# Norm roots on GpSimd, one scaling of the adjacency, a bf16 one-hot, and three VectorE steps on ScalarE, in a four-layer graph network

## The chip, the cores and the metric

The kernel runs on one core of one Trainium2 chip. The metric is the device time of one launch in microseconds, the median of three runs. Engines are named as the profile names them: PE (TensorE; PEld its weight loads), DVE (VectorE), ACT (ScalarE), POOL (GpSimd) and SP (SyncE, which issues all DMAs here).

## The reference

64 graphs of 256 nodes with 128 features go through four layers. The adjacency is 0 or 1, symmetric, with ones on its diagonal, and about one entry in eight is set. Each layer's result is added to its input and normalised over the features.

```python
# layer 0: for each node, the maximum over its neighbours
pre = p[:, :, None, :] + q[:, None, :, :] + b      # p = x (W1 - W2), q = x W2
x = ln(x + max(relu(pre) * adj[..., None], axis=2))
# layer 1: three representations (elu), two aggregated over adj, concatenated
x = ln(x + tanh(concat([adj @ in_rep, node_rep, adj.T @ out_rep]) @ W_upd.T + b_upd))
# layer 2: two graph convolutions with a normalised adjacency
A_hat = adj + eye; deg = A_hat.sum(-1); dinv = where(deg > 0, rsqrt(deg), 0)
norm_A = dinv[..., :, None] * A_hat * dinv[..., None, :]
h = elu(elu(x @ W0 + b0))
h = elu(norm_A @ (h @ W1) + b1)
x = ln(x + norm_A @ (h @ W2) + b2)
# layer 3: a message for every pair, summed over neighbours, and an update
msg = gelu(ln(m_j[:, None] + m_i[:, :, None] + b1) * g1 + be1)
agg = einsum('bijo,bij->bio', msg, adj)
x = ln(x + ln(concat([x, agg]) @ W2 + b2) * g2 + be2)
```

The outer norm is `(x - mean) / sqrt(var + 1e-5)`.

## The kernel before

One graph is one tile of work: its 256 nodes are two halves (`H = 2`) of 128 partitions. The kernel has a path for sparse adjacencies (`sparse`), which this input takes, and a general path behind a flag (`general`), which is built but not run here.

The sparse path doesn't go over all pairs. For each half of the neighbours and each node it lists the neighbours by rank in 40 slots; the nodes are sorted by their number of neighbours, so that later slots are narrower (`RECTS`, 4800 columns in all). A one-hot matrix `hot` in fp8 picks the neighbours by a matmul: `q3` times `hot` for layer 0 (L665, with `pick`/`lack` matmuls L681 that push empty places down, and `fold` with a maximum, L492) and `c3` times `hot` for layer 3 (L728). In layer 3 `sums_of` makes up to 1024 columns at a time: evict and add `dT` (L732, DVE), square (L736, ACT), sum over the features by a matmul with ones (L743), `row` (L745, ACT), out to DRAM as a `line`, back as 16 columns (`vr`), root, reciprocal and a product with `fulls` (L768, L769), out again (L771) and back as `rs_s`, spread over the partitions (L828). `last` then multiplies (L839, DVE), takes the Gelu (L841, ACT), and folds with a sum.

Each tile goes through four stages: `first` (the sorting, `perm`, `hot`, layer 0), `second` (layer 1), `third` (layer 2 and the start of layer 3) and `last`. Four tiles are under way at a time, one in each stage. `together` takes steps of the four generators in turn by their weights, and a scheduler then orders the instructions of each engine by its own estimates. So the order on an engine is fixed when the program is built, each engine works through its list in order, and an instruction that waits holds all behind it.

The steps that the change touches:

- `inverse_root` (L72 to L75): Sqrt on ACT and reciprocal on DVE, on the spot. It is called by `layernorm` (L176, on `rs`, 128x2; five norms a tile), by `layer_2` (L272, on `dinv`) and by `sums_of` (L768, on `vr`). ACT keeps one table of functions at a time; where the function's table isn't there the profile shows an ACT_TABLE_LOAD with the line of the instruction that follows it. Copy, Identity, Square, Sign, Abs and Relu have no such loads of their own here.
- `layer_2` (L261): degree to `dinv`, the identity added to `aT` in place (L277), and per step the hidden state `hs` multiplied by `dinv` (L293, DVE), the matmul with `aT` (L296, PE), a copy (L299), a matmul, and `dinv` and the bias on the way out (L308).
- `elu` (L187): Exp on ACT (L194), for the first hidden layer a second one (L198), and two DVE instructions (L200, L201).
- `first`: `nz`, the adjacency in bf16 (L509, DVE, from `an` that a DMA brings, L507); `diff`, for the flag (L511); the number of neighbours `pc` (L534); four Sign activations that count a node's place (L551); `perm`, the one-hot of the permutation (L560, DVE), in fp32 and read in bf16 through every second half-word (`as_bf16`, L561); matmuls with it (L566, L577) and the copy `nzp` (L571); `full`, ones where a slot is filled (L615, DVE). `perm` is read in fp32 by `third` (L810).
- `layer_1`: `nd`, the node representation with its bias (L233, DVE), then its `elu`.

Of the kernel before, what the change touches and what calls it, by code (L numbers as in the profile page):

```python
# [9 lines left out]
F32 = mybir.dt.float32  # L10
BF16 = mybir.dt.bfloat16
AF = mybir.ActivationFunctionType
ALU = mybir.AluOpType
# [6 lines left out]
P = 128  # L20
# [23 lines left out]
def kernel(  # L44
# [9 lines left out]
    nc = tc.nc  # L54
    B, N, D = x.shape
    assert N == 2 * P and D == P
    H = N // P
    Q = P // 4

    consts = ctx.enter_context(tc.tile_pool(name="consts", bufs=1))  # L60
# [7 lines left out]
    nc.vector.memset(eps_t, EPS)  # L68
    minus1 = consts.tile([P, 1], F32, name="minus1")
    nc.vector.memset(minus1, -1.0)  # L70

    def inverse_root(t):  # L72

        nc.scalar.activation(t, t, AF.Sqrt)  # L74
        nc.vector.reciprocal(t, t)  # L75
# [29 lines left out]
    b1_node = column(l1_b_node, "b1_node")  # L105
# [16 lines left out]
    with tc.tile_pool(name="prep", bufs=1) as prep, tc.tile_pool(  # L122
        name="ps_prep", bufs=2, space=bass.MemoryType.PSUM
# [33 lines left out]
    class Shared:  # L157
# [53 lines left out]

        def node_tile(self, name):
            return self.state.tile([P, H, P], F32, name=name)

        def layer_1(self, s, an, aT, x1):

            work, psum, elu = self.work, self.psum, self.elu
# [15 lines left out]
            nc.vector.tensor_scalar(nd, pn[:, :N], b1_node, None, ALU.add)  # L233
# [27 lines left out]
        def layer_2(self, s, aT, deg_of):  # L261
# [3 lines left out]
            deg = work.tile([P, H], F32, name="deg")  # L265
            deg_of(deg)
            nc.vector.tensor_scalar(deg, deg, 1.0, None, ALU.add)
            pos = work.tile([P, H], F32, name="pos")
            nc.vector.tensor_scalar(pos, deg, 0.0, None, ALU.is_gt)
            dinv = work.tile([P, H], F32, name="dinv")  # L270
            nc.vector.tensor_scalar(dinv, deg, 1e-30, None, ALU.max)
            inverse_root(dinv)  # L272
            yield
            nc.vector.tensor_mul(dinv, dinv, pos)
            for h in range(H):
                blk = aT[:, h, h * P:(h + 1) * P]
                nc.vector.tensor_add(blk, blk, ident)  # L277
            yield
# [12 lines left out]
            for step in (1, 2):  # L291
                for h in range(H):
                    nc.vector.tensor_scalar(hs[:, h], hs[:, h], dinv[:, h:h + 1], None, ALU.mult)  # L293
# [60 lines left out]
    def sparse(ctx):  # L354
# [14 lines left out]
        iota_k = cs.tile([P, N], F32, name="iota_k")  # L369
        down = cs.tile([1, N], BF16, name="down")  # L370
# [19 lines left out]
        with tc.tile_pool(name="cs_prep", bufs=1) as pp:  # L390
# [7 lines left out]
            nc.vector.tensor_copy(iota_k, t)  # L398
            t = pp.tile([P, 1], I32, name="part_i")
# [73 lines left out]
        def as_bf16(t):  # L473

            return t.bitcast(BF16).rearrange("... (n two) -> ... n two", two=2)[..., 1]
# [26 lines left out]
        def first(g, s):  # L502
# [6 lines left out]
            nc.vector.tensor_scalar(nz, an, 1.0, None, ALU.is_equal)  # L509
# [33 lines left out]
            dg = state.tile([P, H], F32, name="dg", bufs=3)  # L543
            nc.vector.tensor_reduce(dg, pc, AX.X, ALU.add)
            s["dg"] = dg
# [11 lines left out]
            perm = state.tile([P, H, H, N], F32, name="perm", bufs=3)  # L557
            for h in range(H):
                for hi in range(H):
                    nc.vector.tensor_scalar(perm[:, h, hi], iota_k, pos[:, h, hi:hi + 1], None, ALU.is_equal)  # L560
            perm_b = as_bf16(perm)  # L561
# [53 lines left out]
            nc.vector.tensor_scalar(full, lack, 0.0, None, ALU.is_equal)  # L615
# [102 lines left out]
        def sums_of(s, i):  # L718
# [49 lines left out]
            inverse_root(vr[:rows])  # L768
# [13 lines left out]
        def third(g, s):  # L782

            dg = s["dg"]

            def deg_of(deg):
                nc.vector.tensor_scalar(deg, dg, 1.0 / N, None, ALU.mult)

            yield from sh.layer_2(s, s["aT"], deg_of)
            yield  # L790
            x3, perm = s["x3"], s["perm"]
# [103 lines left out]
    def general(ctx):  # L895
# [82 lines left out]
        def middle(g, s):  # L978
# [10 lines left out]
            def deg_of(deg):  # L989
                nc.vector.tensor_reduce(deg, an, AX.X, ALU.add)  # L990

            yield from sh.layer_1(s, an, aT, s["x1"])
            yield
            yield from sh.layer_2(s, aT, deg_of)
# [148 lines left out]
```

## Time and profile before

| | |
|---|---|
| runs | 5717.65, 5735.95 and 5736.4 us, median 5735.95 |
| the profiled execution | 5731.62 us, its span 5729.7 us |
| mean granted TensorE clock | 0.862 |
| PE / DVE / ACT / POOL busy | 4529.9 / 4834.4 / 4275.2 / 1.9 us |
| ACT_TABLE_LOAD, by the line behind it | L841 535, L74 445, L194 221, L198 32; 1283 ns each |
| L74 on `rs`, `vr`, `dinv` | 320, 320 and 64 activations, 0.20 to 0.22 us |
| DMA | 365.15 MB, mean 64 GB/s |

Busy times are sums over the whole span, in which all 64 tiles stand one behind the other, with four under way at a time. PE's is modelled, since matmuls are pipelined. The windows view gives the busy time of each engine in any stretch with the clock that TensorE was granted in it, the timeline gives the instructions in order, with the time that the engine was idle before them and what ended it.

### The profile page before, as it was taken

The page shows a single profiled execution, that of the slowest core. Times are in us where ns is not written, and L with a number is a line of the kernel's source. Part 1 is how long each engine was busy: PE and PEld are TensorE (multiplying, and loading weights), DVE is VectorE, ACT ScalarE, POOL GpSimd, SP SyncE. Part 2 cuts the span into 40 slices and gives each one's busy share as a digit, 9 for nine tenths or more (in the row PEclk, how much of TensorE's full clock was granted, in tenths as well). Part 3 has the DMA queues.
Part 4 walks back from the last instruction along what each step waited for, and adds up shares of the span by engine and source line. Part 5 has one row for each costly group of instructions (what it writes and reads, how often), then busy time and mean ns, then how long its engine had stood idle before and what let it go on. Part 6 is the DMA issues. An engine that isn't in the chain of part 4 may idle for free.

```text
span 5729.7 us, 83531 instructions
## 1 busy us (share of the span) xinstructions
PE 4529.9 (79%) x27408; PEld 2508.7 (44%) x27408; DVE 4834.4 (84%) x14654; ACT 4275.2 (75%) x6485; POOL 1.9 (0%) x10
## 2 busy tenths in 40 slices
PE   5878878878778778788788788787887887877875
PEld 2444444444444444444444444444444444444443
DVE  6788888888888888888888888888888888888876
ACT  2577777777777777777777777777777777777785
POOL 0000000000000000000000000000000000000000
PEclk8888889889889889888898898898888887888986
DMA  0122222222212221221221222122212212221222
GB/s 22 44 70 63 62 63 72 62 63 66 69 57 70 65 63 63 72 63 62 63 72 62 63 65 70 59 68 65 63 62 72 64 62 63 69 66 60 68 65 74
DMA packets 292813, 365.15 MB, mean 64 GB/s; under 512 B 151952, under 2 KB 210448, under 8 KB 292368
## 3 DMA queue, kind: packets, MB, share of 16 engines
q1 hardware_dynamic: 292368, 359.73, 20.0%
q8 instruction: 217, 3.56, 0.3%
q14 instruction: 228, 1.87, 0.1%
HBM read 345.07 MB, written 14.53 MB: 63 GB/s over the span
## 4 chain that ended last, share of the span: by engine, by line
PE 52%; DVE 29%; ACT 11%; issue 4%; DMA 3%; SPq 0%; DVEq 0%; POOL 0%; ACTq 0%
PE bigp L665 11%; PE bigp L728 8%; DVE pre L839 6%; PE mm L860 5%; DVE lanes L492 4%; PE mm L743 4%; DVE hot L629 4%; DVE pre L732 4%; DVE sums L492 3%; PE bigp L681 3%; DMA rs_s<-scale_line 2%; PE mm L870 2%; PE mm L296 2%; PE mm L699 2%; PE mm L647 2%
## 5 line engine op out<-in xcount | busy, mean ns | idle before, releaser
L665 PE MATMUL bigp<-hot,q 128*128 128x512 fp8e4 (+1 forms) x3840 | 1052.3, 371 | 66.6 <-DVE lanes L492 52.6
L728 PE MATMUL bigp<-hot,c 128*128 128x512 fp8e4 (+1 forms) x3840 | 928.8, 372 | 140.2 <-DVE pre L732 140.2
L732 DVE TENSOR_TENSOR pre<-bigp,dT 128x512 f32<-128x512 f32 (+6 forms) x1664 | 846.3, 530 | 37.8 <-PE bigp L728 33.5
L492 DVE TENSOR_TENSOR lanes<-bigp,lanes 128x512 f32<-128x512 f32 (+6 forms) x1536 | 772.7, 503 | 94.6 <-PE bigp L681 86.9
L839 DVE TENSOR_TENSOR pre<-pre,rs_s 128x1024 f32<-128x1024 f32 (+1 forms) x640 | 732.9, 1150 | 48.6 <-DMA rs_s<-scale_line 48.0
L736 ACT ACTIVATE sq<-pre 128x1024 f32<-128x1024 f32 (+1 forms) x640 | 638.5, 998 | 169.9 <-DVE pre L732 163.9
L841 ACT ACT_TABLE_LOAD x535 | 686.4, 1283 | 9.5
L492 DVE TENSOR_TENSOR sums<-pre,sums 128x1024 f32<-128x1024 f32 (+6 forms) x1024 | 628.8, 614 | 41.2 <-ACT pre L841 40.7
L745 ACT ACTIVATE row<-mm,eps_t 128x256 f32<-128x256 f32 (+1 forms) x640 | 289.6, 453 | 476.9 <-PE mm L743 476.7
L841 ACT ACTIVATE pre<-pre,be,g 128x1024 f32<-128x1024 f32 (+1 forms) x512 | 594.2, 1172 | 57.8 <-DVE pre L839 53.0
L743 PE MATMUL mm<-sq,ones 128*32 128x256 f32 (+1 forms) x5120 | 482.9, 440 | 135.2 <-ACT sq L736 135.2
L74 ACT ACT_TABLE_LOAD x445 | 570.9, 1283 | 7.5
L728 PEld LDWEIGHTS <-c 128*128 128x128 bf16 x3840 | 331.2, 98 | 550.5 <-issue 136.1
L665 PEld LDWEIGHTS <-q 128*128 128x128 bf16 x3840 | 310.8, 97 | 392.6 <-issue 112.0
L296 PE MATMUL mm<-aT,hs 128*128 128x256 f32 x512 | 232.3, 600 | 316.1 <-DVE hs L293 214.8
L629 DVE TENSOR_SCALAR hot<-rank 128x512 fp8e4<-128x512 bf16 (+5 forms) x1536 | 440.5, 348 | 0.0
L681 PEld LDWEIGHTS <-pick 42*128 42x128 bf16 x2944 | 155.8, 95 | 481.5 <-issue 474.2
L296 PEld LDWEIGHTS mm<-aT,hs 128*128 128x128 f32 x512 | 135.6, 293 | 425.8 <-issue 316.1
L860 PE MATMUL mm<-w3u,sums 128*128 128x128 f32 x2048 | 296.7, 289 | 18.4 <-DVE sums L492 16.1
L194 ACT ACT_TABLE_LOAD x221 | 283.5, 1283 | 3.9
L681 PE MATMUL bigp<-lack,pick 42*128 42x36 bf16 (+16 forms) x2944 | 285.7, 187 | 0.0
L860 PEld LDWEIGHTS mm<-w3u,sums 128*128 128x128 f32 x2048 | 254.5, 195 | 37.3 <-issue 17.6
(226 smaller groups left out, 7132.6 us busy)
## 6 DMA issues: line engine op xcount, KB each, us to landing
rs_s<-scale_line SPq DMA_DIRECT2D x512, 512.0 KB
rs_s<-scale_line SPq DMA_DIRECT2D x128, 352.0 KB
an<-in_adj SPq DMA_DIRECT2D x64, 256.0 KB
x<-in_x SPq DMA_DIRECT2D x64, 128.0 KB
line<-row SPq DMA_DIRECT2D x512, 4.0 KB
out<-o SPq DMA_DIRECT2D x64, 128.0 KB
fu<-fulls SPq DMA_DIRECT2D x192, 4.0 KB
vr<-line SPq DMA_DIRECT2D x192, 8.0 KB
```

Source lines behind the costliest of these rows:

```text
L74: nc.scalar.activation(t, t, AF.Sqrt)
L492: nc.vector.tensor_tensor(lanes[:, :k, :w], src[:, i:i + k], lanes[:, :k, :w], op)
L629: nc.vector.tensor_scalar(hot[:, :, at:at + w], rank[:, :, :w], s0 + i + 1.0 - FAR, None, ALU.is_equal, saturate=False)
L665: nc.tensor.matmul(pt[:, :tl], q3[:, i, h], hot[:, h, t0:t0 + tl], start=i == 0, stop=False)
L681: nc.tensor.matmul(o_, l_, r_, start=False, stop=i == len(todo) - 1)
L728: nc.tensor.matmul(pt[:, :bl], c3[:, k, h], hot[:, h, t0 + b:t0 + b + bl], start=k == 0, stop=k == 2)
L732: nc.vector.tensor_add(block(pre[:, b:], n, w, at), block(pt, n, w, at), widen(dT[:, h, :w], n))
L736: nc.scalar.activation(sq[:, :tl], pre[:, :tl], AF.Square)
L743: nc.tensor.matmul(pr[q * Q:(q + 1) * Q, :tl // 4], ones[:, :Q], v4[:, :, q], start=True, stop=True)
L839: nc.vector.tensor_mul(pre[:, :tl], pre[:, :tl], rs[:, :tl])
L841: nc.scalar.activation(msg[:, :tl], pre[:, :tl], AF.Gelu, bias=be3, scale=g3)
L860: nc.tensor.matmul(pt[:, cols], lanes[:, k, cols], w3u[:, 1], start=k == 0, stop=False)
```

## The change

Six edits, and what goes with them:

- `inverse_root` becomes one POOL instruction, the power -0.5 (`mhalf` holds the exponents). `vr` keeps Sqrt and reciprocal, now written out in `sums_of`.
- `dinv` is made by a new `inverse_root_of`, in the sparse path in `first` right after `pc`, and kept for `third` (four buffers); its product with `pos` is on POOL.
- In `layer_2` the rows of `aT` are multiplied by `dinv` once per tile, after the identity is added; the two products of `hs` go.
- `perm` is made in bf16 from a bf16 `iota_b`, without the half-word view; `third` makes an fp32 copy `perm_f` on ACT for its matmul.
- `nz` is a copy on ACT instead of a comparison on DVE.
- `nd` is an Identity activation with bias, and `full` a Relu of 1 - `lack`, both on ACT instead of DVE.

```diff
     def inverse_root(t):
-        nc.scalar.activation(t, t, AF.Sqrt)
-        nc.vector.reciprocal(t, t)
+        nc.gpsimd.tensor_tensor(t, t, mhalf[:t.shape[0], :t.free_size()], ALU.pow)
...
+        def inverse_root_of(self, deg, bufs):
+            nc.vector.tensor_scalar(deg, deg, 1.0, None, ALU.add)
+            pos = self.work.tile([P, H], F32, name="pos")
+            nc.vector.tensor_scalar(pos, deg, 0.0, None, ALU.is_gt)
+            dinv = self.state.tile([P, H], F32, name="dinv", bufs=bufs)
+            nc.vector.tensor_scalar(dinv, deg, 1e-30, None, ALU.max)
+            inverse_root(dinv)
+            nc.gpsimd.tensor_mul(dinv, dinv, pos)
+            return dinv
...
             nd = work.tile([P, N], F32, name="nd")
-            nc.vector.tensor_scalar(nd, pn[:, :N], b1_node, None, ALU.add)
+            nc.scalar.activation(nd, pn[:, :N], AF.Identity, bias=b1_node)
...
             for h in range(H):
                 blk = aT[:, h, h * P:(h + 1) * P]
                 nc.vector.tensor_add(blk, blk, ident)
+            for h in range(H):
+                nc.vector.tensor_scalar(aT[:, h], aT[:, h], dinv[:, h:h + 1], None, ALU.mult)
...
             for step in (1, 2):
-                for h in range(H):
-                    nc.vector.tensor_scalar(hs[:, h], hs[:, h], dinv[:, h:h + 1], None, ALU.mult)
                 pa = psum()
...
-            nc.vector.tensor_scalar(nz, an, 1.0, None, ALU.is_equal)
+            nc.scalar.copy(nz, an)
...
-            dg = state.tile([P, H], F32, name="dg", bufs=3)
+            dg = work.tile([P, H], F32, name="dg")
             nc.vector.tensor_reduce(dg, pc, AX.X, ALU.add)
-            s["dg"] = dg
+            nc.vector.tensor_scalar(dg, dg, 1.0 / N, None, ALU.mult)
+            s["dinv"] = sh.inverse_root_of(dg, 4)
...
-            perm = state.tile([P, H, H, N], F32, name="perm", bufs=3)
+            perm = state.tile([P, H, H, N], BF16, name="perm", bufs=3)
             for h in range(H):
                 for hi in range(H):
-                    nc.vector.tensor_scalar(perm[:, h, hi], iota_k, pos[:, h, hi:hi + 1], None, ALU.is_equal)
-            perm_b = as_bf16(perm)
+                    nc.vector.tensor_scalar(perm[:, h, hi], iota_b, pos[:, h, hi:hi + 1], None, ALU.is_equal)
+            perm_b = perm
...
-            nc.vector.tensor_scalar(full, lack, 0.0, None, ALU.is_equal)
+            nc.scalar.activation(full, lack, AF.Relu, bias=one_t[:ROWS], scale=-1.0)
...
-            inverse_root(vr[:rows])
+            nc.scalar.activation(vr[:rows], vr[:rows], AF.Sqrt)
+            nc.vector.reciprocal(vr[:rows], vr[:rows])
...
-            x3, perm = s["x3"], s["perm"]
+            x3 = s["x3"]
+            perm = work.tile([P, H, H, N], F32, name="perm_f")
+            nc.scalar.copy(perm, s["perm"])
```

The general path gets the same `inverse_root_of`; it isn't run here. The constants `mhalf`, `one_t` and `iota_b` are made once.

More of the change, by code (lines that the diff above doesn't have):

```diff
@@ L68 @@
     nc.vector.memset(eps_t, EPS)
+    one_t = consts.tile([P, 1], F32, name="one_t")
+    nc.vector.memset(one_t, 1.0)
     minus1 = consts.tile([P, 1], F32, name="minus1")
     nc.vector.memset(minus1, -1.0)
+    mhalf = consts.tile([P, 16], F32, name="mhalf")
+    nc.vector.memset(mhalf, -0.5)
     def inverse_root(t):
-        nc.scalar.activation(t, t, AF.Sqrt)
-        nc.vector.reciprocal(t, t)
+        nc.gpsimd.tensor_tensor(t, t, mhalf[:t.shape[0], :t.free_size()], ALU.pow)
     def load(src, shape, name):
@@ L259, in layer_1, with layer_2 @@
             s["x2"] = x2
-        def layer_2(self, s, aT, deg_of):
+        def layer_2(self, s, aT, dinv_of):
             work, psum, elu = self.work, self.psum, self.elu
             x2 = s["x2"]
[L265 to L272, printed above, removed]
+            dinv = dinv_of()
             yield
-            nc.vector.tensor_mul(dinv, dinv, pos)
             for h in range(H):
@@ L369, in sparse @@
         iota_k = cs.tile([P, N], F32, name="iota_k")
+        iota_b = cs.tile([P, N], BF16, name="iota_b")
         down = cs.tile([1, N], BF16, name="down")
@@ L398, in sparse @@
             nc.vector.tensor_copy(iota_k, t)
+            nc.vector.tensor_copy(iota_b, t)
             t = pp.tile([P, 1], I32, name="part_i")
@@ L782, in third @@
         def third(g, s):
[L784 to L789, printed above, removed]
+            yield from sh.layer_2(s, s["aT"], lambda: s["dinv"])
             yield
-            x3, perm = s["x3"], s["perm"]
+            x3 = s["x3"]
+            perm = work.tile([P, H, H, N], F32, name="perm_f")
+            nc.scalar.copy(perm, s["perm"])
             x3T = sh.to_features(x3, "x3T")
@@ L987, in middle, with dinv_of @@
             yield
-            def deg_of(deg):
+            def dinv_of():
+                deg = work.tile([P, H], F32, name="deg")
                 nc.vector.tensor_reduce(deg, an, AX.X, ALU.add)
+                return sh.inverse_root_of(deg, 1)
             yield from sh.layer_1(s, an, aT, s["x1"])
             yield
-            yield from sh.layer_2(s, aT, deg_of)
+            yield from sh.layer_2(s, aT, dinv_of)
             yield
```

## Prediction

> **What bounds the kernel now.** I read the totals first, then the windows over one tile's period, then the order of time inside it. A tile's period is the distance between two `nzp` copies (L571): seven of them start at 2925.4 to 3448.6 us, so 523.2 / 6 = 87.2 us; 64 tiles of that and the fill make the span of 5729.7 us. The totals show no full engine:
>
> ```profile
> PE 4529.9 (79%) x27408; PEld 2508.7 (44%) x27408; DVE 4834.4 (84%) x14654; ACT 4275.2 (75%) x6485; POOL 1.9 (0%) x10
> ```
>
> The average hides three stretches with different limits. The windows show them (columns: window, length, busy us of PE, its weight loads, DVE, ACT, POOL, then the granted TensorE clock, DMA share, GB/s):
>
> ```profile
> 3003.00:3032.00 29.00, 17.86 (x80) 10.41 (x73) 21.54 (x68) 23.85 (x38) 0.00 (x0) 0.50 0.20 58
> 3032.00:3082.00 50.00, 49.32 (x328) 27.32 (x327) 44.68 (x138) 35.90 (x53) 0.00 (x0) 1.00 0.21 67
> 3082.00:3091.00 9.00, 4.22 (x29) 1.74 (x27) 8.86 (x22) 7.99 (x12) 0.00 (x0) 0.94 0.18 44
> ```
>
> In the middle 50 us PE is full at full clock: what DVE or ACT lose there is worth nothing. In the tail (9 us) DVE is full. In the front (29 us) PE idles 11 us and its clock is at 0.50, and ACT works through its list. There the clock is also what idling costs: four L296 matmuls take 2.08 us at 3028. The timeline of ACT shows what the front waits for:
>
> ```profile
> 3014.99 1.28 ACT L198 ACT_TABLE_LOAD   x1
> 3016.28 0.51 ACT L198 ACTIVATE elu_e<-elu_e,minus 128x256 f32<-128x256 f32 x1
> 3016.70 1.04 ACT L736 ACTIVATE sq<-pre 128x1024 f32<-128x1024 f32 x1
> 3017.76 1.28 ACT L841 ACT_TABLE_LOAD   x1
> 3019.05 1.24 ACT L841 ACTIVATE pre<-pre,be,g 128x1024 f32<-128x1024 f32 x1
> 3020.31 1.28 ACT L194 ACT_TABLE_LOAD   x1
> ```
>
> Three functions (Exp, Gelu, Sqrt) change places, and each change is a load of 1.28 us. This tile pays two loads around the second Exp (L198). In the next tile that Exp runs at 3097.36, before the Gelu, with no load of its own. The `nzp` distances are 86.0 us (2925.42 to 3011.43) and 88.9 us (to 3100.33): tiles alternate, and the order with the extra loads costs 2.9 us more. The tail's chain ends in the norm that makes `x1`:
>
> ```profile
> 3084.68 0.16 DVE L174 TENSOR_SCALAR rs<-mv 128x2 f32<-128x2 f32 x1
> ...
> 3087.24 0.11 DVE L75 RECIPROCAL rs<-rs 128x2 f32<-128x2 f32 x1
> ...
> 3087.93 0.60 DVE L180 TENSOR_SCALAR x<-y,mv,rs 128x128 f32<-128x128 f32 x2
> ```
>
> From variance to result are 3.25 us, since the root stood behind a Gelu and a load on ACT (3086.01), and PE waits 2.04 us for L180.
>
> **The change part by part.** The order of the built program tells what stands where.
>
> Roots: 320 `rs` and 64 `dinv` roots leave ACT (64.4 + 13.0 us), and their reciprocals DVE (48.6 + 9.4). In the built order ACT's loads fall from 1236 to 892: 344 x 1.283 = 441 us. But per tile (19.5 to 14) nearly all of it lies in the middle. From the Gelu of the tail (3082.17) to the hidden layer's Exp (3111.60 in the faster kind of tile) there were 8 loads; after, 9, because the `vr` root with its load now stands ahead of that Exp. So 441 us of ACT time are worth almost nothing as such. The row has the next ACTIVATE 0.01 us behind a load's end. The Trainium skill (ScalarE: Activation LUTs, "What ACT_TABLE_LOAD costs") adds a drain of 1380 ns to 1283 ns; no gap here shows it, and with it ACT's relief would be estimated at 344 x 2.66 = 915 us, in the same stretch.
>
> POOL: seven small instructions a tile (five `rs`, the `dinv` power and its product). No trace row has a power. Low end: the 128x1 IOTA, 0.13 us; high end: 3.25 us, today's whole way; nearest are POOL's rows of 0.13 to 0.45 us, and I take 0.5 us with both semaphore hops. Behind the `x1` and `o` variances DVE has only one or two instructions (about 0.6 us) before it needs the root, so at 0.5 it doesn't wait; behind the others 1.2 to 2.3 us. `x1` then comes 3.25 - 0.8 = about 2.5 us earlier. Of this I count 1.0 us: the tail's Gelu (its input product now follows `o` and `y` on DVE, over 1 us later) and ACT's full list behind it keep the rest.
>
> A rule against the change stands in SBUF — State Buffer, "Who interferes with whom": GpSimd and VectorE share a port pair, and one that holds it blocks the other wholly, when VectorE reads two SBUF tensors or runs in a two-port mode. No run shows it yet, as POOL was idle. By it, seven holds of an estimated 0.3 us would be 2 us of DVE a tile.
>
> The order: in all steady tiles of the built program the second Exp now precedes the Gelu; 87.2 - 86.0 = 1.2 us a tile.
>
> ACT's new work in the front: `full` (42x512, as L591's row 0.69 us), the `vr` load and root ahead of the Exp (1.28 + 0.20): +2.2 us. `nd` on ACT (0.47, L745's row) lies behind that Exp and saves the load before its own (1.28); at nothing, hidden by the L296 matmuls, 0.5 if these get faster.
>
> DVE in the front: from Exp's end (3112.03) to PE's L296 (3114.21) went 2.2 us, with folds, `vr` and two L293 between. Without L293 (0.18 + 0.28) and with the `vr` pair put ahead, what is left is L200 0.29 + L201 0.42 and hops, 0.8: -1.4 us.
>
> Adjacency: 256 x 0.270 (L293) = 61 us leave DVE; 128 products of 128x256 (L560's form, 0.347) = 44 us come, in the middle, where DVE has 5 of 50 us free; 0.7 us a tile if that cover goes. The four small steps to `dinv` (0.16 us each) move from 3054 and 3072 to just after the `pc` sums (3003), where DVE waits 2.84 us for L223: nothing.
>
> One-hot: 256 instructions of 0.347; a bf16 form between 0.270 (L293, half the elements) and 0.347: I take 0.28, 17 us. PE starts at the first of four, and ACT's Gelu ahead of `nzp` ends later: nothing. `perm_f` is a new ACT copy of 1024 columns (L736's 1.05 us, 67 us in all), a period ahead of its matmul, in the middle: nothing; 1 us if ACT were late there.
>
> `nz` from DVE (0.42) to ACT (about 0.6, L540's row) is the one move with a new wait. It now stands ahead of the `x3T` copy, some 9 us earlier in the tile than on DVE. Its input can be fetched only when L240 has read the old `an` (ends 3040.8); the fetch's packets end 4.1 to 6.4 us after the issue, so at 3045 to 3047, while ACT gets there at 3045.3. Behind it wait `x3T`, L797 and PE. SP also has this fetch ahead of two 512 KB `rs_s` transfers, which then start up to 2 us later; DVE's slack hides them. I take +0.2 us, bounds 0 and 1.8.
>
> Sum: -1.2 + 2.2 - 1.0 - 1.4 + 0.2 = -1.2, and -0.1 for what the reciprocals (0.15 us each) leave free in the tail: -1.3 us a tile; 62 tiles' worth with the fill: -81. The profiled execution is 5731.62 us (span 5729.7), 4.3 below the median 5735.95. So 5736 - 81 = 5655.
>
> **The rivals.** (1) Slower: the power on POOL is long. Each us above 0.6 is waited for twice in the full tail, once by `o` and once by `x1`, DVE standing with all that follows. It eats the gain at 0.6 + 1.3/2 = 1.25 us; at 2 us it is 2.8 - 1.3 = +1.5 a tile, 5736 + 93 = 5829; at 1.6, 5780. For it: no row bounds a power from above. Against: two elements a partition, and every POOL row is under 0.5 us.
> (2) No change: ACT waits on `an` (1.8 instead of 0.2 us): 5736 + 62 x 0.3 = 5755, or half of that, 5705. For it: the times above nearly touch. Against: the fetch now stands ahead of the `rs_s` issues that delayed it.
> (3) The front follows `x1` wholly: 2.5 instead of 1.0 us, and PE's clock rises there: -2.8 to -3.3 a tile, 5532 to 5562. Against it speaks ACT's list, 23.85 busy of 29 us.
> That the change doesn't do what it says: the loads do fall in the built order; it is excluded there.
>
> **How the numbers follow.** What a measurement here can tell from no change is about 0.5%, 29 us: faster is below 5707, slower above 5765. Forecast, 5590 to 5706: 0.50, all faster. (3): 0.15, faster. (2): 0.13, of it 0.03 faster, 0.08 same, 0.02 slower. (1): 0.22, of it 0.02 same. Sums: 0.68, 0.10, 0.22. The range goes from 5545, within (3), to 5790, within (1). Likeliest own range: 5590 to 5706.
>
> **What would show it.** Right: ACT loads x381, x318 and x189; an `nzp` distance near 86 us in every tile; the middle still at clock 1.00 and full; POOL `rs` rows of 0.2 to 0.6 us, and `x` after its variance in about 0.8 to 1.0. Wrong: POOL rows over 1 us with DVE idle for them (rival 1); ACT `nz` with idle time from the DMA of over 1 us a tile and PE idle at the w3c matmul (rival 2); a period under 85 us with a front clock well above 0.65 (rival 3).

## The result and the profile after

The changed kernel takes 5813.49 us (median of four runs, 5810.92 to 5814.92) against 5729.93 us for the kernel before in the same comparison: ratio 1.0144, 95% interval 1.0124 to 1.0164. It is slower by some 84 us, where 81 us of gain were forecast. The profiled execution took 5814.14 us, its span 5812.0.

The page's totals:

```profile
PE 4568.7 (79%) x27408; PEld 2550.3 (44%) x27408; DVE 4746.0 (82%) x13889; ACT 3948.4 (68%) x6013; POOL 281.6 (5%) x458
```

ACT is spared 327 us and DVE 88 us, and the table loads fell to 892 as the built order had it (L849 381, L778 318, L198 189), yet the span grew by 82 us. So less busy time on ACT and DVE didn't shorten the run.

To see where the time went I cut each tile at two events that every kernel here has: ACT's copy `m` at the end of layer 0 (L705 before, L715 after) and ACT's copy `q` behind which the next tile's layer 0 starts on PE (L497, L506). From `m` to `q` is the **front** (in the prediction's terms the tail and the front), from `q` to `m` the **middle**. The lengths below are means over 48 steady tiles of the profiled execution, from the start times in the timelines; PE idle is the time within the stretch in which no matmul ran.

| | front | middle | PE idle in the middle | tile |
|---|---|---|---|---|
| before | 38.39 | 48.81 | 1.38 | 87.2 |
| changed | 38.46 | 50.29 | 2.82 | 88.7 |

The front, where 1.3 us of gain were forecast, stayed; the middle, where nothing was to happen, took 1.5 us more, and that is the whole loss (1.5 us x 62 tiles = 93 us, against 84 measured). One tile of the changed kernel in the windows view (columns as in the prediction; first the front, then the middle):

```profile
3033.85:3072.17 38.32, 23.20 (x117) 12.49 (x117) 30.04 (x90) 32.70 (x53) 2.26 (x4) 0.70 0.18 56
3072.17:3122.84 50.67, 47.51 (x317) 27.12 (x320) 43.53 (x125) 29.10 (x43) 2.07 (x3) 0.99 0.22 70
```

The middle is at clock 0.99 and nearly full, 47.51 of 50.67 us. But "nearly" is the point: 3.2 us of PE idle stand in it. The groups of PE's lines show for whom PE waits, first before, then after (last part: idle time before the group, and what ended it):

```profile
L665 PE MATMUL bigp<-hot,q 128*128 128x512 fp8e4 (+1 forms) x3840 | 1052.3, 371 | 66.6 <-DVE lanes L492 52.6 <-DVE q L499 11.0 <-DVE pre L732 1.1
L296 PE MATMUL mm<-aT,hs 128*128 128x256 f32 x512 | 232.3, 600 | 316.1 <-DVE hs L293 214.8 <-DVE vr L769 101.3
L207 PE MATMUL mm<-ident,x 128*128 128x128 f32 x512 | 148.8, 356 | 107.8 <-DVE x L180 107.8
...
L743 PE MATMUL mm<-sq,ones 128*32 128x256 f32 (+1 forms) x5120 | 482.9, 440 | 135.2 <-ACT sq L736 135.2
L585 PE MATMUL mm<-nzp,upto 128*128 128x512 bf16 x64 | 38.2, 596 | 1.9 <-ACT nzp L571 1.9
```

```profile
L675 PE MATMUL bigp<-hot,q 128*128 128x512 fp8e4 (+1 forms) x3840 | 1073.7, 373 | 180.1 <-DVE lanes L501 144.3 <-DVE pre L742 27.3 <-DVE q L508 7.9
L303 PE MATMUL mm<-aT,hs 128*128 128x256 f32 x512 | 265.5, 674 | 219.7 <-DVE hs L205 219.7
L211 PE MATMUL mm<-ident,x 128*128 128x128 f32 x512 | 148.2, 361 | 12.2 <-DVE x L184 12.2
...
L753 PE MATMUL mm<-sq,ones 128*32 128x256 f32 (+1 forms) x5120 | 467.9, 443 | 207.5 <-ACT sq L746 207.5
L595 PE MATMUL mm<-nzp,upto 128*128 128x512 bf16 x64 | 37.3, 582 | 75.9 <-ACT nzp L581 75.9
```

The gains in front did arrive at PE: 96 us less wait for `x1` (L207, L211) and 96 us less for `hs` (L296, L303). But other waits of the front took their place: 74 us more for `nzp`, 72 for the squares `sq`, and 45 for the evictions `pre` ahead of layer 3's matmuls (140.2 us at L728, 184.8 at L738), 191 us in all. So PE's idle time in the front is 15.0 us a tile instead of 15.7, and the front is as long as it was. In the middle 113 us more wait stands before the layer 0 matmuls, 92 of it for the fold into `lanes`. The timeline shows how that comes about (DVE and PE, in the middle of the same tile):

```profile
3097.68 0.69 DVE L501 TENSOR_TENSOR lanes<-bigp,lanes 128x512 f32<-128x512 f32 x1 [0.51 <-ACT pre L849]
...
3098.29 1.22 DVE L501 TENSOR_TENSOR sums<-pre,sums 128x1024 f32<-128x1024 f32 x1
...
3099.42 0.68 DVE L501 TENSOR_TENSOR lanes<-bigp,lanes 128x512 f32<-128x512 f32 x1
...
3100.03 1.22 DVE L501 TENSOR_TENSOR sums<-pre,sums 128x1024 f32<-128x1024 f32 x1
...
3101.16 1.22 DVE L847 TENSOR_TENSOR pre<-pre,rs_s 128x1024 f32<-128x1024 f32 x1
...
3102.29 0.68 DVE L501 TENSOR_TENSOR lanes<-bigp,lanes 128x512 f32<-128x512 f32 x1
...
3103.03 0.81 PE L675 MATMUL bigp<-hot,q 128*128 128x512 fp8e4 x3 [1.15 <-DVE lanes L501]
```

The q matmuls write into four PSUM tiles `bigp`, which they share with layer 3's matmuls; DVE's fold into `lanes` or its eviction into `pre` frees one. Here two 1024-column sums of layer 3 (`sums`, from another tile) and a product (L847) stand between three folds, 3.66 us of them, and PE stands 1.15 us for the third. Nothing in this is new work: the sums, the product and the folds are those of the kernel before, with the same durations. They stand in another order, since the scheduler laid out all engines' lists anew. The kernel before has two kinds of tile that alternate; at the same place in the kind with less PE idle in the middle (0.83 us, against 1.91 in the other), one product and no sum stands between the second and the third fold:

```profile
3056.54 0.68 DVE L492 TENSOR_TENSOR lanes<-bigp,lanes 128x512 f32<-128x512 f32 x1
...
3057.98 0.69 DVE L492 TENSOR_TENSOR lanes<-bigp,lanes 128x512 f32<-128x512 f32 x1 [0.27 <-PE bigp L681]
...
3058.79 1.21 DVE L839 TENSOR_TENSOR pre<-pre,rs_s 128x1024 f32<-128x1024 f32 x1
...
3059.91 0.68 DVE L492 TENSOR_TENSOR lanes<-bigp,lanes 128x512 f32<-128x512 f32 x1
```

The power on POOL, and the way from the last variance to `x1`:

```profile
L79 POOL TENSOR_TENSOR rs<-rs,mhalf 128x2 f32<-128x2 f32 x320 | 223.1, 697 | 5152.1 <-DVE rs L178 4656.6 <-DVE lanes L501 495.6
```

```profile
3127.64 0.16 DVE L178 TENSOR_SCALAR rs<-mv 128x2 f32<-128x2 f32 x1
...
3127.95 0.69 POOL L79 TENSOR_TENSOR rs<-rs,mhalf 128x2 f32<-128x2 f32 x1 [3.44 <-DVE rs L178]
...
3128.67 0.60 DVE L184 TENSOR_SCALAR x<-y,mv,rs 128x128 f32<-128x128 f32 x2 [0.28 <-POOL rs L79]
```

From variance to `x1` are 1.03 us instead of 3.25, near the 0.8 to 1.0 us of the forecast. The power's row is 0.70 us, above the 0.2 to 0.6 us that were named as a sign of being right, and DVE waits 38 us for POOL in the whole run, 0.6 us a tile where nothing was counted.

ACT's list in the front, the lines that answer to the loads shown before:

```profile
3056.54 0.71 ACT L625 ACTIVATE full<-lack,one_t 42x512 bf16<-42x512 bf16 x1
3057.26 1.28 ACT L198 ACT_TABLE_LOAD   x1
3058.56 0.63 ACT L198 ACTIVATE elu_e<-io 128x512 f32<-128x512 f32 x1
...
3064.27 1.28 ACT L778 ACT_TABLE_LOAD   x1
3065.56 0.21 ACT L778 ACTIVATE vr<-vr 108x16 f32<-108x16 f32 x1
3065.80 1.28 ACT L198 ACT_TABLE_LOAD   x1
3067.09 0.42 ACT L198 ACTIVATE elu_e<-hs 128x256 f32<-128x256 f32 x1
```

`full` stands ahead of the Exp of `io`, and the `vr` root with its load ahead of the hidden Exp (3067.09), for which PE then waits. The second Exp stands before the Gelu in every tile, as the order said.

### The profile page after: what moved, and what is told of

Same layout as the page of the kernel before. It is cut to its first block, busy times and chain, and to the rows that moved or that the text cites. A ratio compares the mean times of both kernels' runs of the same rounds, so it can differ in the third digit from the quotient of the medians.

```text
span 5812.0 us, 82528 instructions
## 1 busy us (share of the span) xinstructions
PE 4568.7 (79%) x27408; PEld 2550.3 (44%) x27408; DVE 4746.0 (82%) x13889; ACT 3948.4 (68%) x6013; POOL 281.6 (5%) x458
## 4 chain that ended last, share of the span: by engine, by line
PE 51%; DVE 20%; ACT 17%; DMA 5%; issue 4%; POOL 2%; SPq 0%; POOLq 0%; DVEq 0%; ACTq 0%
PE bigp L675 12%; PE bigp L738 8%; DVE pre L847 5%; PE mm L868 4%; DVE pre L742 4%; DMA rs_s<-scale_line 4%; PE bigp L691 3%; ACT L198 3%; ACT pre L849 3%; PE mm L753 3%; ACT L849 3%; DVE lanes L501 3%; DVE sums L501 2%; ACT sq L746 2%; PE mm L303 2%
## 5 line engine op out<-in xcount | busy, mean ns | idle before, releaser
L675 PE MATMUL bigp<-hot,q 128*128 128x512 fp8e4 (+1 forms) x3840 | 1073.7, 373 | 180.1 <-DVE lanes L501 144.3
L738 PE MATMUL bigp<-hot,c 128*128 128x512 fp8e4 (+1 forms) x3840 | 989.9, 385 | 184.8 <-DVE pre L742 184.6
L847 DVE TENSOR_TENSOR pre<-pre,rs_s 128x1024 f32<-128x1024 f32 (+1 forms) x640 | 728.5, 1139 | 73.2 <-DMA rs_s<-scale_line 73.0
L849 ACT ACTIVATE pre<-pre,be,g 128x1024 f32<-128x1024 f32 (+1 forms) x512 | 600.5, 1174 | 62.3 <-DVE pre L847 58.2
L753 PE MATMUL mm<-sq,ones 128*32 128x256 f32 (+1 forms) x5120 | 467.9, 443 | 207.5 <-ACT sq L746 207.5
L738 PEld LDWEIGHTS <-c 128*128 128x128 bf16 x3840 | 347.3, 101 | 616.1 <-DVE pre L742 220.9
L79 POOL TENSOR_TENSOR rs<-rs,mhalf 128x2 f32<-128x2 f32 x320 | 223.1, 697 | 5152.1 <-DVE rs L178 4656.6
L303 PE MATMUL mm<-aT,hs 128*128 128x256 f32 x512 | 265.5, 674 | 219.7 <-DVE hs L205 219.7
L303 PEld LDWEIGHTS mm<-aT,hs 128*128 128x128 f32 x512 | 150.4, 324 | 339.3 <-DVE hs L205 246.7
```

The source lines that it names most:

```text
L303: nc.tensor.matmul(pa[:, :N], hs[:, h], aT[:, h], start=h == 0, stop=h == H - 1)
L675: nc.tensor.matmul(pt[:, :tl], q3[:, i, h], hot[:, h, t0:t0 + tl], start=i == 0, stop=False)
L738: nc.tensor.matmul(pt[:, :bl], c3[:, k, h], hot[:, h, t0 + b:t0 + b + bl], start=k == 0, stop=k == 2)
L753: nc.tensor.matmul(pr[q * Q:(q + 1) * Q, :tl // 4], ones[:, :Q], v4[:, :, q], start=True, stop=True)
L847: nc.vector.tensor_mul(pre[:, :tl], pre[:, :tl], rs[:, :tl])
L849: nc.scalar.activation(msg[:, :tl], pre[:, :tl], AF.Gelu, bias=be3, scale=g3)
```

## The experiments

Each group of kernels was run beside the kernel before, whose median was 5726.5 to 5730.9 us there. Front, middle and half clock are of each kernel's profiled execution; half clock is the time per tile in which the granted TensorE clock was 0.5.

| run | us | ratio, 95% interval | front | middle | half clock |
|---|---|---|---|---|---|
| before | 5729.9 | | 38.39 | 48.81 | 22.5 |
| changed | 5813.5 | 1.0144 (1.0124 to 1.0164) | 38.46 | 50.29 | 26.1 |
| e1 roots alone | 5698.8 | 0.9950 (0.9931 to 0.9968) | 37.61 | 49.14 | 23.8 |
| e2 changed, roots back | 6013.8 | 1.0505 (1.0483 to 1.0527) | 41.06 | 51.06 | 30.7 |
| e3 changed, one-hot back | 5815.3 | 1.0158 (1.0137 to 1.0180) | 38.47 | 50.27 | 25.9 |
| e4 nz, nd, full alone | 5892.9 | 1.0292 (1.0269 to 1.0315) | 41.55 | 48.54 | 28.0 |
| e5 changed, these three back | 5778.1 | 1.0076 (1.0050 to 1.0103) | 36.80 | 51.81 | 30.0 |
| e6 changed, nz back | 5781.8 | 1.0097 (1.0069 to 1.0124) | 38.44 | 49.75 | 25.7 |
| e7 changed, full back | 5729.0 | 1.0009 (0.9988 to 1.0030) | 36.65 | 50.78 | 27.3 |
| e8 all roots on POOL | 6018.4 | 1.0506 (1.0478 to 1.0533) | 44.10 | 47.66 | 30.5 |
| e9 e1, filled twice | 5800.2 | 1.0130 (1.0109 to 1.0151) | 38.67 | 49.72 | 16.6 |
| e10 changed, filled twice | 5831.2 | 1.0187 (1.0166 to 1.0209) | 38.89 | 49.86 | 13.8 |
| e11 e7, filled twice | 5802.8 | 1.0140 (1.0117 to 1.0163) | 38.50 | 50.03 | 16.5 |
| e12 e1 and full | 5728.4 | 1.0000 (0.9988 to 1.0012) | 38.29 | 48.88 | 23.8 |
| e13 e1, perm gap filled | 5677.2 | 0.9914 (0.9898 to 0.9931) | 37.23 | 49.04 | 17.5 |
| e14 changed, aT on POOL | 5815.5 | 1.0150 (1.0133 to 1.0167) | 38.48 | 50.26 | 25.9 |
| e15 e7, aT on POOL | 5719.3 | 0.9981 (0.9971 to 0.9992) | 36.66 | 50.27 | 25.9 |
| e16 e8, product on POOL | 5944.6 | 1.0376 (1.0359 to 1.0393) | 42.59 | 48.10 | 27.0 |
| e17 roots, nd, scaling | 5622.2 | 0.9819 (0.9806 to 0.9833) | 36.83 | 48.65 | 24.7 |
| e18 e17, aT on POOL, gap filled | 5618.2 | 0.9810 (0.9797 to 0.9824) | 36.63 | 48.70 | 16.2 |

### Which part costs

**e1**, the kernel before with

```diff
 def inverse_root(t):
-    nc.scalar.activation(t, t, AF.Sqrt)
-    nc.vector.reciprocal(t, t)
+    nc.gpsimd.tensor_tensor(t, t, mhalf[...], ALU.pow)
```

> The kernel before with one edit: the roots of the norms and of the degrees on GpSimd (the vr root stays on ScalarE). Theory 'plan': the changed kernel lost its time in the middle of the period because the built order of VectorE and ScalarE was laid out anew once the Sqrts left ScalarE; the order built here has the same long L492 sums and L839 products between the folds of `lanes` in every tile, so the loss stays: 5780 to 5830 us, PE idle before the q matmuls (L665) for `lanes` at 100 us or more in sum against 53 before. Rival 'work': the loss comes from the work that the other edits put on ScalarE (nz, nd, full, perm_f: 64 x (0.61 + 0.47 + 0.71 + 1.04) = 181 us), which makes the nzp copy and the squares late; without it the gain of the front shows: 5640 to 5700 us, PE idle for nzp under 10 us. Rival 'root late': VectorE waits for the power (0.70 us) wherever a norm stands; it would give the same time as 'plan', but with over 100 us of VectorE idle time put down to POOL.

Measured 5698.8 us, inside the range of "work" near its upper end, but without its sign: the wait for `nzp` is 62 us, not under 10. The roots gain 28 us, not 81, and don't lose. `lanes` is waited for 96 us (53 before), near the 100 of "plan", so a part of the middle's loss is there already. "Root late" is out: DVE's time waiting for the power stays as small as in the changed kernel.

**e2**, the changed kernel with the old `inverse_root` back.

> The changed kernel with the roots back on ScalarE (Sqrt) and VectorE (reciprocal); all other edits stay. 'Plan': the built order has no such run of sums between the folds of `lanes` (one product of 512 columns stands there instead), the second Exp stands ahead of the Gelu in every tile: near 86 to 87.3 us a tile, 5650 to 5735 us. 'Work': ScalarE carries its old Sqrts with their loads and the four new pieces, so it is slower than the kernel before and than the changed one: 5790 to 5900 us.

Both numbers were too low; that it is slower than both kernels is as "work" had it. In this built order the early `dinv` root, now on ACT, brings its load between the Signs of the front, and from the `m` copy to `nzp` takes 22.07 us instead of 19.64. With the roots on ACT the other edits lose; the run tells nothing on the changed kernel's own loss.

**e3**, the changed kernel with `perm` in fp32 and without `perm_f`.

> The changed kernel with the one-hot back in fp32, so without perm_f (1.04 us a tile on ScalarE). The built order of VectorE around `lanes` is the same as in the changed kernel. 'Plan': 5795 to 5820 us, PE idle for `lanes` near 144 us as in the changed kernel. 'Work': a third of the added ScalarE work is gone, the PE waits for nzp (76 us) and for the squares (207 us) shrink by some 60 us together: 5740 to 5770 us.

The time is the changed kernel's, as "plan" had it. PE's waits are nearly the same too: 144.0 us for `lanes`, 64 for `nzp` (76 in the changed kernel) and 207 for the squares. The bf16 one-hot is worth nothing, as forecast.

**e4**, the kernel before with `nz`, `nd` and `full` on ACT.

> The kernel before with nz, nd and full on ScalarE alone. The built order has the second hidden Exp behind the Gelu, with a load of its own, in every tile, where the kernel before has it in every other one, and saves the load ahead of the Exp of nd. 'Plan': the time follows that order, near 88.9 us in every tile, the kernel before's slower kind: 5800 to 5840 us. 'Work': the three pieces cost what they take in the front alone (nd 0.47 and part of nz): 5745 to 5790 us, with nzp distances still alternating.

Slower than either theory had it. The order is as read (61 loads at the second Exp, L200), and the Exp of `io` comes 10.67 us after `nzp` in every tile, as in the slower kind of tile before (10.15; mean of both kinds 7.02); the middle is no longer (48.54). While the Sqrts are still on ACT, ACT's front has no room at all.

**e5, e6 and e7**, the changed kernel with all three, with `nz` alone and with `full` alone back on DVE.

> The changed kernel with nz, nd and full back on VectorE; roots on GpSimd, the single scaling and the bf16 one-hot stay. After the first four runs (roots alone 86.74 us a tile, three parts alone 90.06, the changed kernel 88.74, without the bf16 one-hot 88.75) the loss of 2.0 us a tile against the roots alone lies in the three parts or in the scaling. Theory 'three parts': without them the time falls back to that of the roots alone, 86.5 to 87.1 us a tile, 5685 to 5725 us. Rival 'scaling': the 128 products of aT (39 us of VectorE in the middle, with a long L501 sum still between the folds of `lanes`) are what PE waits for: 88 to 88.7 us a tile, 5770 to 5815 us.

> The changed kernel with nz back on VectorE. In the built order one of the two 1024-column sums that stand between the first folds of `lanes` is gone, perm_f has moved ahead of the squares, full still stands ahead of the Exp of io. Theory 'order of the folds': PE idle for `lanes` falls from 144 to about 100 us, and the time by as much: 5760 to 5785 us. Rival 'full': nothing changes in the front, and the waits in the middle only move from one line to another: 5800 to 5820 us.

> The changed kernel with full back on VectorE. In the built order the vr root with its load then stands behind the hidden Exp instead of ahead of it, the Exp of nd gets its own load back (60 loads more in all), and full's 0.71 us are gone from ahead of the Exp of io. Theory 'full': of the front +0.6 (nzp to Exp of io) and the time that the hidden Exp waits for the vr root go, 1 to 2 us a tile: 5690 to 5755 us. Rival 'scaling or folds': the loss lies in the middle and stays: 5790 to 5820 us.

e7 settles `full`: one ACT instruction of 0.71 us on or off ACT is 84 us. With it the front is 1.81 us a tile longer (36.65 to 38.46) and the middle 0.49 shorter: its own length, and the `vr` root that its place lets slip ahead of the hidden Exp. In e7's middle the second sum stands ahead of the fourth fold instead of the third. PE then waits 96 us for `lanes`, as in e1, but 78 for the evictions `pre` (27 in the changed kernel), and is idle as long, 2.86 us a tile.

e6 is the first sign for the order of the folds: the built order has one sum less between the first folds, which stand as in e1. PE's wait for `lanes` falls from 144 to 102 us, its idle time in the middle from 2.82 to 2.10 us a tile, and the time by 32 us.

e5 misses "three parts" and lies at the lower edge of "scaling": its front falls as with e7, and its folds stand as in e7, but its middle is the longest of all. In 49 of 52 tiles of its profile one window at half clock falls into the middle, which is then 51.95 us long, and 49.75 in the other three. The profiled execution is the longest of its five (5806 us, the others 5757 to 5785), so the table shows its middle at its worst. Edits don't add here, since each lays out the lists anew.

### Does the clock set the front?

Within a kernel the longer tiles tend to have more half clock (before: 26 us in the slower kind, 18 in the faster), so I tried to buy the clock back with matmuls of constants.

```diff
+def warm(pt, n):
+    for _ in range(n):
+        nc.tensor.matmul(pt[:, :N], ident, half, start=True, stop=True)
...
 pz = psum()
+warm(pz, 8)
...
 pa = psum()
+if step == 1: warm(pa, 6)
```

> The kernel with the roots alone (5698.8 us, 86.75 us a tile, of it 23.8 us at half the TensorE clock and 16.5 us of PE idle), plus 14 matmuls of constants (128x256 fp32) a tile whose results are overwritten: eight ahead of the perm matmuls (L566) and six ahead of the first adjacency matmul of layer 2 (L296), into the PSUM tile that these use, where PE waits 3.9 and 2.7 us. ScalarE's built order stays. Theory 'clock': an idle stretch of PE is paid twice, once as such and once as 3.4 us windows at half clock after it; in the traces so far a window at full clock with PE under 0.4 busy is followed by half clock, over 0.6 never, and 0.2 us of period go with each us at half clock. Filled, the half-clock time falls from 23.8 to 12 us or less: 84 to 85 us a tile, 5520 to 5610 us, although PE does more work. Rival 'work': the clock stays, each matmul takes 0.66 us at half clock, so perm's and hs's matmuls come 1.3 us later each: up to 89.4 us a tile, 5780 to 5870 us.

> The changed kernel with the same 14 filling matmuls a tile at the same two places. 'Clock': the half-clock time falls from 26.1 to 14 us or less, the time to 5640 to 5720 us. 'Work': 5890 to 5980 us.

> The changed kernel without full on ScalarE (5729.0 us, its tiles 86.3 us long with 21.2 us at half clock or 88.7 us with 30.7, in one and the same order of instructions), with the same 14 filling matmuls. 'Clock': the long kind of tile goes, all near 84 to 86 us: 5530 to 5640 us. 'Work': 5800 to 5900 us.

Half clock fell by 7 to 12 us a tile, and all three got slower, by 101, 18 and 74 us. The changed kernel's tile is 88.75 us with 13.8 us at half clock and 88.74 with 26.1. That speaks against the clock as what sets the front, but doesn't settle it: the first adjacency matmul has no wait in these kernels (the gap is at the second), so six of the added matmuls stood on the path there and may have cost what the clock gave.

> The roots alone (5698.8 us) with eight filling matmuls ahead of the perm matmuls only. The three filled kernels before (+102, +18 and +74 us against their own kernels, at 7 to 12 us less half clock a tile) had six more ahead of the first adjacency matmul of layer 2, where PE doesn't wait in these kernels; that place cost them some 1 to 1.6 us. Theory 'ScalarE's list': in the stretch from the `m` copy to the `q` copy ScalarE works its list without a break and sets the length, so PE's clock there is worth nothing: half-clock time falls by 4 us or more and the time stays, 5685 to 5715 us. Rival 'clock': the half clock of the front is on the path: 5590 to 5670 us.

Filled only where PE waits (eight matmuls of 0.39 us, PE's wait for `perm` 250 to 12 us), half clock falls by 6.3 us a tile and the time by 22 us, between the two ranges (7 us above "clock", 8 below "ScalarE's list"). The front is 0.4 us shorter: 0.06 us for each us of half clock, where "clock" had 0.2. The stretch from `m` to `nzp` stays at 19.5 us; the 0.4 us come between `nzp` and the Exp of `io`. So the clock counts for little in the front, but for something.

In the middle it is different. Two tiles of e7, the same instructions in the same order, with the same 2.86 us of PE idle:

```profile
2857.00:2909.04 52.04, 49.18 (x317) 28.30 (x320) 43.44 (x125) 29.01 (x43) 2.07 (x3) 0.95 0.25 82
3033.07:3082.71 49.64, 46.78 (x317) 26.58 (x320) 43.25 (x125) 29.18 (x43) 2.07 (x3) 1.00 0.25 86
```

In the longer tile two stretches ran at half clock, 2.0 us at its start and one window of 3.4 us at 39.5 us, and it is 2.4 us longer. There a us of half clock costs 0.4 us, in the front 0.06.

**e12**, e1 with `full` on ACT.

> The roots on GpSimd and full on ScalarE, nothing else of the change. In this built order full stands behind the load of the Exp of io and the vr root behind the hidden Exp, other than in the changed kernel, where both stand ahead. Theory 'place': what full cost (84 us between the changed kernel and the one without it) is its place ahead of the Exps, so here it costs little: 5690 to 5720 us. Rival 'its work': it costs the same anywhere in the front, 5760 to 5790 us.

5728.4 us, between the two, and the mean hides two kinds of tile that alternate. In 24 of 48 `full` stands behind the Exp of `io` and the `vr` root behind the hidden Exp; their front is 37.70 us, 0.09 more than in e1. In the other 24 both stand ahead, as in the changed kernel, and the front is 38.86 us, 1.25 more. So it is the place that costs, as "place" had it; the built order has the good place in every other tile alone. The place behind the Exps also has to make up for 0.56 us that `nzp` comes later in those tiles, in which the powers for `o` and `x1` take 1.53 us instead of 0.69 (shown under "The rules that were weighed").

### Work or order in the middle?

**e14 and e15**, the changed kernel and e7 with

```diff
-nc.vector.tensor_scalar(aT[:, h], aT[:, h], dinv[:, h:h + 1], None, ALU.mult)
+nc.gpsimd.tensor_scalar(aT[:, h], aT[:, h], dinv[:, h:h + 1], None, ALU.mult)
```

> The changed kernel with the 128 products of aT on GpSimd instead of VectorE. The built orders of ScalarE and VectorE stay as they are, but for these products (0.61 us a tile, with the identity added 0.9). Theory 'VectorE's list in the middle': from the first fold of `lanes` on VectorE sets the pace, so what it is spared is spared: 5740 to 5780 us. Rival 'order of the folds': the two 1024-column sums between the folds make PE wait as before, 144 us: 5795 to 5820 us.

> The changed kernel without full on ScalarE (5729.0 us: its front 1.7 us shorter than before, its middle 2.0 us longer) and with the products of aT on GpSimd. 'VectorE's list in the middle': 5640 to 5695 us, the q matmuls' wait for the eviction L732 (78 us) at 40 or less. Rival 'order of the folds': 5715 to 5735 us. Rival 'GpSimd too slow': 128x256 on GpSimd takes over 2 us each, and layer 2 waits for it: over 5760 us.

The rival holds in both. With 39 us of products off DVE and all else in its place, PE still waits 144 us for `lanes` in e14, and the time is the changed kernel's. In e15 it waits 97 us for `lanes` and 78 for the evictions, as in e7, and the time is 10 us less. DVE's added products are not the cause.

**e17**, e1 with `nd` on ACT and the single scaling, but `dinv` made in `layer_2` as before. The products are on DVE, as in the changed kernel; in the built order the second sum no longer stands ahead of the third fold.

> The roots on GpSimd, nd on ScalarE and the single scaling (on VectorE, with dinv made where it was before, in layer 2); full, nz and the one-hot as before. Against the changed kernel without full (5729.0 us, q to m 49.98 us with 2.87 us of PE idle, front 36.65) the built order of ScalarE's front is the same, but the second 1024-column sum no longer stands ahead of the third and fourth folds of `lanes`: the folds stand as with the roots alone (q to m 48.74 us, PE idle 1.67). Theory 'order of the folds': the middle is that of the roots alone and the front that of the kernel without full, 85.4 to 86.0 us a tile: 5610 to 5665 us. Rival 'the added products': the middle stays near 50 us: 5700 to 5730 us.

5622.2 us, as the order theory had it: 104 us under the kernel before in its own comparison (5726.5), 191 under the changed one. The same place in its timeline (`lanes` is L494 here, the layer 0 matmul L667):

```profile
2998.66 1.22 DVE L494 TENSOR_TENSOR sums<-pre,sums 128x1024 f32<-128x1024 f32 x1
...
2999.79 0.68 DVE L494 TENSOR_TENSOR lanes<-bigp,lanes 128x512 f32<-128x512 f32 x1
3000.39 1.21 DVE L842 TENSOR_TENSOR pre<-pre,rs_s 128x1024 f32<-128x1024 f32 x1
3001.53 0.68 DVE L494 TENSOR_TENSOR lanes<-bigp,lanes 128x512 f32<-128x512 f32 x1
3001.72 0.81 PE L667 MATMUL bigp<-hot,q 128*128 128x512 fp8e4 x3
```

One sum and one product between three folds instead of two sums and a product, and PE goes on without a wait. The front (36.83 us) is near that of e7 (36.65), and the middle (48.65) no longer than those of e1 (49.14) and of the kernel before (48.81).

Sorted by where these two sums stand among the folds, fourteen of the kernels fall into three groups by PE's idle time in the middle. With the sums ahead of the second and third fold (changed, e3, e10, e14) it is 2.81 to 2.82 us a tile, ahead of the second and fourth (e5, e7, e11, e15) 2.83 to 2.87, ahead of the first and second (e1, e6, e9, e13, e17, e18) 1.66 to 1.68, and 2.10 in e6. The work on the engines differs within each group. No run changed the order and nothing else.

**e18** adds the products of `aT` on POOL and the filled perm gap.

> The run before it with the products of aT on GpSimd and eight filling matmuls ahead of the perm matmuls, the two steps that gained 10 and 22 us in earlier runs. 'Steps add': 5575 to 5635 us, and faster than all kernels so far. Rival 'a product on GpSimd (0.93 us) is late for layer 2 in this order' or 'the fill takes what the clock gives': not below the run before it.

4 us below e17, which the intervals don't tell apart: half clock falls from 24.7 to 16.2 us a tile and the time stays. The steps don't add. Both beat the two kernels of the case.

### All roots on POOL

**e8** is e1 with the `vr` power on POOL, **e16** has its product with `fulls` there too.

```diff
-nc.scalar.activation(vr[:rows], vr[:rows], AF.Sqrt)
-nc.vector.reciprocal(vr[:rows], vr[:rows])
-nc.vector.tensor_mul(vr[:rows], vr[:rows], fu[:rows])
+inverse_root(vr[:rows])
+nc.gpsimd.tensor_mul(vr[:rows], vr[:rows], fu[:rows])      # e8: nc.vector
```

> The roots alone on GpSimd as in the first run, with the vr root (108x16) there too: no Sqrt is left on ScalarE, and the loads fall from about 954 to about 400. Theory 'loads in the front count, those in the middle don't': of the some 9 loads that fall per tile only the one or two in the front count, 1 to 3 us a tile, if the power of 16 elements stays under 2 us: 5500 to 5640 us. Rival 'the power is long': the power grows with its elements (2 take 0.69 us, so 16 could take up to 5.5 us), the scale line comes later, and VectorE waits for rs_s: 5700 to 5800 us.

> The eighth run (all roots on GpSimd, 6018 us, VectorE waiting 779 us for the vr power of 3.07 us) with the product of vr and fulls on GpSimd as well, so that VectorE has no part in it. Theory 'head of the line': what cost the eighth run its time was VectorE standing at that product with all its other work behind it; gone, the 835 loads fewer show: 5530 to 5640 us. Rival 'the scale line is late': the power delays rs_s and with it L839 by 3 us in each group, VectorE waits for that instead: 5750 to 5950 us.

The loads fall to 379 and 381, and the kernels are 289 and 214 us slower than the kernel before. The power of 16 elements takes 3 us, and whoever needs its result next has all its other work behind it. In e8 that is DVE at the product, in e16 DVE at L841, waiting for `rs_s` (groups of POOL and DVE in e8, then of DVE in e16):

```profile
L77 POOL TENSOR_TENSOR vr<-vr,mhalf 128x16 f32<-128x16 f32 x192 | 582.7, 3035 | 275.6 <-DMA vr<-line 161.2 <-DVE sums L494 61.8 <-DVE elu_e L202 33.4
```

```profile
L771 DVE TENSOR_TENSOR vr<-vr,fu 128x16 f32<-128x16 f32 (+1 forms) x320 | 56.1, 175 | 779.2 <-POOL vr L77 779.2
```

```profile
L841 DVE TENSOR_TENSOR pre<-pre,rs_s 128x1024 f32<-128x1024 f32 (+1 forms) x640 | 737.2, 1152 | 464.2 <-DMA rs_s<-scale_line 463.3
```

e16 is as its rival had it, in number and mechanism. e8's rival was right that the power is long, but the time is 218 us above its range, and DVE stands at the product and not at `rs_s`. A relief of over 1000 us on an engine (857 and 855 loads) doesn't pay for 12 and 7 us a tile (779 and 464 us) of standing at the head of another engine's list. In e16 the powers for `o` and `x1` also take 1.60 us instead of 0.70 in nearly every tile, which is a part of its loss.

## Why the prediction was wrong

**The step that failed first: the middle, put at nothing.** The prediction says "In the middle 50 us PE is full at full clock: what DVE or ACT lose there is worth nothing", and its sum has no term for the middle. PE was full there because DVE's folds and evictions came just in time for four PSUM tiles, not because DVE didn't matter. The view showed 49.32 of 50 us and I read it as slack for the others; DVE had 44.68 of 50, and a list in which its long instructions bunch up makes PE wait. Measured: PE idle in the middle 1.38 to 2.82 us, the middle 1.48 us longer. e14 excludes the added products, and the idle time goes with the order of the folds in fourteen kernels. I read the built order for ACT and for the front, and didn't read DVE's in the middle, where the second sum ahead of the third fold could be seen. Why the scheduler puts it there was not settled.

**The front, forecast at -1.3, measured 0.** Term by term:

- The order of the second Exp, -1.2: in the kernel before, the fronts of the two kinds of tile are 37.59 and 39.26 us. With the roots alone (e1) all tiles have the order of the faster kind, and the front is 37.61: -0.8. The faster tiles' period of 86.0 us holds only beside slower ones: e1's is 86.75.
- `x1` 2.5 us earlier, counted -1.0: it comes 2.2 us earlier (3.25 to 1.03) and PE waits 1.5 us a tile less for it, yet e1's front is that of the faster kind before: nothing. The step held that ACT's full list keeps the rest; it keeps all. This is the most mis-sized term of the front.
- The way to L296, -1.4: PE waits 1.5 us a tile less at L303, though the Exp itself comes later. The front of e7, which has this and not `full`, is 0.96 us shorter than e1's.
- ACT's new work, +2.2: the changed kernel against e7, +1.81. Right in kind and nearly in size.
- `nz`, +0.2: ACT waits for `an` 29.5 us in all, four times; nothing in steady tiles. But its move changed DVE's order, and with `nz` back on DVE (e6) the time is 32 us less.

The gains of -1.2, -1.0, -1.4 and -0.1 with `nz` at +0.2 sum to -3.5; without `full` the front gave -1.74 (e7). Gains that meet on one list, ACT's, were added as if each lay on the path by itself.

**The rivals.** (1) had the sign, but not the mechanism of the loss: the power takes 0.70 us, 0.87 from the variance's end to `x1`'s norm, where I took 0.5 with its hops, and the break-even was 1.25. What it says of twice the time above 0.6 us does show: DVE waits 0.6 us a tile for POOL. (2) and (3) fell. That adjacency, one-hot and `perm_f` cost nothing by themselves was right (e3, e14): the bf16 one-hot takes 282 ns as estimated.

**The rules that were weighed.** The Trainium skill's rule that POOL and DVE block each other at their shared port when VectorE reads two SBUF tensors (SBUF — State Buffer, "Who interferes with whom") shows on POOL's side. L847's product reads two SBUF tensors. In the changed kernel three of the 320 `rs` powers begin while it runs and take 1.53 to 1.59 us; beside folds and evictions, which read PSUM, they take 0.69 (as at 3127.95 above). In e12 it is 61 of 320, with 1.53 us, in e16 119, with 1.60. One of those of e12, where the product is L844:

```profile
2993.67 1.22 DVE L844 TENSOR_TENSOR pre<-pre,rs_s 128x1024 f32<-128x1024 f32 x1
2993.91 1.53 POOL L79 TENSOR_TENSOR rs<-rs,mhalf 128x2 f32<-128x2 f32 x1 [4.40 <-DVE rs L178]
```

The 0.84 us more are near the 0.98 us that the product still runs after the power's start. DVE isn't held: its product takes 1209 ns after, 1216 before, and 1219 in e16, where POOL is busy 1480 us. So the 2 us of DVE a tile that the prediction estimated by the rule don't show; what the rule costs depends on where the list puts the power, and in the changed kernel it is next to nothing. The drain behind a table load (ScalarE: Activation LUTs, "What ACT_TABLE_LOAD costs") doesn't show: the Exp at 3058.56 starts 0.02 us after its load's end.

## What to carry to other kernels

A stretch in which one engine is 98% busy is not slack for the engines that feed it: ask how many buffers lie between them, and read the feeder's order there as closely as on the path. In a program whose lists are laid out by a scheduler, an edit has two prices, its work and the new order, and the second can be the larger; price each edit alone, then the combination, and keep those whose lists stay good (here the roots, `nd` and the scaling: 5622 us). Relief on an engine counts only in the stretch where its list is the path, and gains that all end on that list don't add.

## What the runs showed of the hardware

- A power on POOL takes 0.69 us for 128x2 fp32, and 1.53 to 1.60 where it begins while DVE works on two SBUF operands (the product with `rs_s`); 3.0 us for 128x16; a product there 0.19 us for 128x2; a product of 128x256 by a column 0.93 us, against 0.31 on DVE.
- TensorE's clock changes in windows of 3.41 us. In the traces before and after all 248 windows at full clock with PE busy under 0.35 were followed by one at half clock, and 8 of 1920 with PE busy over 0.55, the highest at 0.76 (the "never" over 0.6 in e9's expectation is too strong). From half clock it came back only after a window with PE busy over 0.75, and mostly over 0.85. So 2.2 us of idle time in a window cost the clock in every case. The Trainium skill (TensorE: Matmul & The Clock Gate, "Terms") prices throttled time at half of it. The runs come near that only where PE sets the pace: e7's two tiles differ by 2.4 us for 5.4 us of half clock in the middle, while e13's tiles have 6.3 us less of it than e1's, nearly all in the front, and are 0.5 us shorter.
